# Six blocks of P and four units in flight, results by ScalarE and GpSimd, and the looks at w1 and w2 last

## The chip, the cores and the metric

The kernel runs on one core of a Trainium2 chip. The metric is the device time of one execution in microseconds. A core has TensorE (PE in the profile, its weight loads PEld), VectorE (DVE), ScalarE (ACT), GpSimd (POOL) and SyncE (SP), each working through its own instructions in order, and 16 DMA engines that serve the transfers issued by the queues of SyncE, ScalarE and GpSimd.

## The reference

The input x has 2 batches of 2048 rows of 256. The output is x plus causal attention with one head plus a gated feed-forward network whose weights are ternary (-1, 0 or 1, with one scale for each output):

```python
xn = layernorm(x)
s = where(causal, (xn @ Wq) @ (xn @ Wk).T, -max) * 256 ** -0.5
a = softmax(s) @ (xn @ Wv) @ Wo
h = silu(tlin(xn, w1)) * tlin(xn, w2)       # tlin(x, w) = x @ w.T * s ; 256 -> 1024
h = gelu(tlin(h, h1)); h = gelu(tlin(h, h2))  # 1024 -> 1024
out = x + a + tlin(h, w3)                   # 1024 -> 256
```

## The kernel before

**Two parts.** The kernel computes the attention for all rows first, and the feed-forward network (`ffn_ternary`) after it. In between stands one branch: beside the attention the kernel looks at the weights and counts what would make them not ternary; the sum is `flag`, and a general `ffn` runs where it isn't zero. Numbers are carried as a high and a low half, so that a product takes several matmuls.

**The attention's order.** The rows are cut into 8 blocks n of 512 rows (four for each batch, `NB = 4`), and each block into 4 tiles t of 128 queries. A tile (n, t) meets the key blocks m of its batch up to n. The batch of n = 0..3 is done from the last tile down to the first, that of n = 4..7 upwards, so there are 32 tiles. Python loops write out the order by hand: a list of scoring steps of tile j and a list of weighing steps of tiles some way behind are merged by their TensorE cost (`merged`).

**Scoring.** `score` makes six matmuls for each 512 keys (L401); VectorE moves the scores to SBUF and takes the maximum (L410); when the tile's keys are complete ScalarE takes the exponentials (L422).

**Turning.** P must lie with the keys on the partitions. For most blocks VectorE transposes 32x32 blocks of up to 8 x 128 keys, a *unit* of two key blocks (`turn_blocks`, L292), SyncE stores them to DRAM (d), and four transfers fetch them back in the turned order (`fetch_blocks`, L304) into a tile e; there are 2 such tiles. `turn` then casts the high half of one block (ScalarE, L460) and subtracts for the low half (L462, on VectorE for even m, on GpSimd for odd m) into a tile pT of the pool `ptp`, which holds `LEAD + 2` = 4 of them. Short units go through TensorE transposes instead (L466). `weigh_steps` turns blocks up to `LEAD` = 2 ahead of the one being weighed; `fetch_units` fetches a unit when its first block is turned.

**Weighing.** `weigh` accumulates P times V over a tile's blocks in one PSUM tile po of two halves: one matmul of 512 columns for each 128 keys with the high half of P (L480) and one of 256 with the low half (L485). There are two po. After the last block VectorE sums up and inverts the denominators, ScalarE scales the second half (y, L495), VectorE scales the first and adds y (r, L499), and SyncE stores r of a whole block n (L504).

**Keys and norms.** For the second batch `start_keys` has GpSimd apply the norm (L320), 16 instructions of 128x256 between about 75 and 101 us; `keys` then casts on ScalarE (L338) and subtracts on GpSimd (L339).

**The looks.** `beside(cost)` lets one step of a second list, `looks`, go each time TensorE has been given some cost of work. The list holds, in this order before the change: w1 and w2 (`low`: rounding into w1_sb and w2_sb by GpSimd, L134, then VectorE L558 and ScalarE L560), for each of four pairs of chunks of h1 the sums of factors (VectorE L153) and two `odd` (ScalarE's Abs L565 and VectorE's L567, 128x1024 each), then h2 and parts of w3. When the list is empty, the flag is made by one matmul and copied (L742 to L745). At the end `values_load` (L1173) and the branch (L1174) stand on all engines.

**The feed-forward network.** Each product of 1024 x 1024 factors is done with seven products of half the size instead of eight (`STEPS`). TensorE has eight PSUM banks in two sets of four (`ps_tiles` and `own`); `banks(k)` hands out a set as a whole (k = 4) or as a pair. L172 is the gated product of w1 and w2, L181 and L186 its evictions into f and its halves, L848 the products of h1 and h2.

Of the kernel before, what the change touches and what calls it, by code (L numbers as in the profile page):

```python
# [20 lines left out]
P = 128  # L21
TB = 512
# [10 lines left out]
LOOKS_FROM = 3  # L33
LEAD = 2
WARM = 14

# [28 lines left out]
def attn_ffn_kernel(  # L65
# [123 lines left out]
    with ExitStack() as actx:  # L189
# [6 lines left out]
        sp = actx.enter_context(tc.tile_pool(name="sp", bufs=3))  # L196
        bp = actx.enter_context(tc.tile_pool(name="bp", bufs=2))
        ptp = actx.enter_context(tc.tile_pool(name="ptp", bufs=LEAD + 2))
        small = actx.enter_context(tc.tile_pool(name="small", bufs=4))
# [3 lines left out]
        xs, rstds, ks, qs, vs = {}, {}, {}, {}, {}  # L203
        turns = {"ps": 0, "b": 0, "q": 0}

# [4 lines left out]
        def bank():  # L210
            return in_turn("ps", ps_tiles)

        def load_x(n):
# [40 lines left out]
        def weights_product(name, aT, b, factor):  # L254

            r = cp.tile([P, DC, 2, D], F32R, name=name)
            for c in range(DC):
                ps = bank()
                for d in range(DC):
                    nc.tensor.matmul(  # L260
                        out=ps[:, :D], lhsT=aT[:, d, ts(c, P)], rhs=b[:, d, :],
                        start=(d == 0), stop=(d == DC - 1),
                    )
                f = rp.tile([P, D], F32, tag="y", name=f"wf_{name}_{c}")
# [47 lines left out]
        def start_keys(n):  # L312
            xt = xs.pop(n)
            if n not in rstds:
                mv = cp.tile([P, NT, 2], F32, name=f"mv_{n}")
                stats(xt, mv, n)
                rstds[n] = root(mv, NT, str(n))
            rstd, off = rstds[n]
            for t in range(NT):
                nc.gpsimd.tensor_scalar(  # L320
                    xt[:, t, :], xt[:, t, :], rstd[:, t : t + 1], off[:, t : t + 1],
                    ALU.mult, ALU.add,
                )
            return xt
# [113 lines left out]

        def fetch_units(until, more):
            while units and (more or until not in fetched):  # L440
                more = more and until not in fetched
                n, t, u, k, d = units.pop(0)
                e = bp.tile([P, UK * P], F32, tag="e", name=f"e_{n}_{t}_{u}")[:, : k * P]
                fetched[n, t, u] = fetch_blocks(d, k, e)

        def turn(n, t, m):
# [3 lines left out]
            w = tiles * P  # L450
            pT = ptp.tile([P, 2, TB], F32R, tag="pT", name=f"pT_{n}_{t}_{m}")
            state[n, t][m] = pT
            if by_blocks(n, t, m):
                u, at = divmod((m - first) * NT, UK)
                fetch_units((n, t, u * UK), at == 0)
                src = fetched[n, t, u * UK][:, ds(at, tiles)]
                hi, lo = (
                    pT[:, a, :w].rearrange("p (k i q) -> p k i q", k=tiles, q=Q) for a in range(2)
                )
                nc.scalar.copy(hi, src)  # L460
                engine = nc.gpsimd if m % 2 else nc.vector
                engine.tensor_tensor(lo, src, hi.bitcast(F32), ALU.subtract)  # L462
                return
# [5 lines left out]
            hi_lo(pT[:, 0, :w], pT[:, 1, :w], pt[:, :w])  # L469

        def weigh(n, t, m):
            first = n - n % NB
            st = state[n, t]
# [15 lines left out]
            if m == n:  # L489
# [3 lines left out]
                nc.vector.reciprocal(inv, total)  # L493
                y = rp.tile([P, D], F32, tag="y", name=f"y_{n}_{t}")
                nc.scalar.activation(y, st["po"][:, 1, :], AF.Copy, scale=inv)  # L495
                if n not in attn:
                    attn[n] = rp.tile([P, NT, D], F32, tag="r", name=f"r_{n}"), []
                r, made = attn[n]
                nc.vector.scalar_tensor_tensor(  # L499
                    r[:, t, :], st["po"][:, 0, :], inv, y, ALU.mult, ALU.add  # L500
                )
                made.append(t)
                if len(made) == NT:
                    nc.sync.dma_start(out=r_d[n], in_=r.rearrange("p t d -> p (t d)"))  # L504
                del state[n, t]
# [8 lines left out]
        def weigh_steps(g, until):  # L514

            steps = []
            while g < len(blocks) and blocks[g][0] <= until:
                while turned[0] <= min(g + LEAD, len(blocks) - 1) and (
                    turned[0] <= g or blocks[turned[0]][0] <= until + 1
                ):  # L520
                    b = blocks[turned[0]]
                    steps.append((0 if by_blocks(*b[1:]) else 2 * TB, lambda b=b: turn(*b[1:])))
                    turned[0] += 1
                _, n, t, m = blocks[g]
                steps.append((6 * TB if m < n else 6 * P * (t + 1), lambda b=blocks[g]: weigh(*b[1:])))
                g += 1
# [67 lines left out]
        def item_factors(src, f, c):  # L594
# [3 lines left out]
                (1500, lambda t: store_sums(f, c)),  # L598
                (1500, lambda t: odd(t[0])),
                (3000, lambda t: odd(t[1])),  # L600
# [118 lines left out]
        j = -1  # L719
        checked = False  # L720
        while until < len(tiles) - 1:
# [16 lines left out]
            merged(a, b, beside)  # L738
            if not looks and not checked:
                checked = True  # L740
                most = small.tile([P, 1], F32, tag="most", name="most")
                nc.vector.reduce_max(most, low_bits[:, : looked[0]], axis=AX.X)  # L742
                pf = bank()
                nc.tensor.matmul(out=pf[:1, :1], lhsT=most, rhs=ones, start=True, stop=True)
                nc.vector.tensor_copy(flag, pf[:1, :1])  # L745

        assert checked
        last_quarter = [bank(), bank()]
# [3 lines left out]
    def ffn_ternary(actx):  # L752
# [467 lines left out]
```

## Time and profile before

| what | value |
|---|---|
| median of 3 runs | 872.24 us (872.12 to 873.47) |
| the profiled execution | 871.0 us, of which the span is 869.1 us |
| mean granted TensorE clock | 0.993 |
| TensorE busy | 851.9 us, 98% of the span |
| VectorE, ScalarE, GpSimd busy | 645.9, 498.6 and 236.1 us |
| attention until the first gated product of the last step | to 280.74 us |

Times in the profile are microseconds from the start of the span. A group is named by its line, engine, operation and tiles, as in `L499 DVE ... r<-po,inv,y`. "Releaser" (<-) is what ended the idle time before an instruction. Successive matmuls overlap, so the mean duration of one in the profile is longer than its share of TensorE: the starts of the 512-column matmuls lie 0.227 us apart.

### The profile page before, as it was taken

To read this page: it belongs to the slowest core of one execution; us is meant where nothing else is said; L and a number is where in the kernel's file an instruction comes from. 1 tells how busy PE (TensorE), PEld (TensorE's weight loads), DVE (VectorE), ACT (ScalarE), POOL (GpSimd) and SP (SyncE) were. 2 spreads that over 40 slices of the span, in tenths; PEclk is the share of its full clock that TensorE was granted. 3 is DMA by queue.
4 is the path that set the end of the run, shared out by engine and by line. 5 is a ranking of instruction groups with operands and counts; after the bars stand their busy time and mean duration, and the time that the engine had idled before them with its cause. 6 is when DMAs were issued, how large, how long until landed. Compare 5 with 4: busy or idle time off the path is not lost.

```text
span 869.1 us, 12231 instructions
## 1 busy us (share of the span) xinstructions
PE 851.9 (98%) x4280; PEld 720.8 (83%) x4280; DVE 645.9 (74%) x1127; ACT 498.6 (57%) x881; POOL 236.1 (27%) x180
## 2 busy tenths in 40 slices
PE   8999989999999999999999999999999999999997
PEld 5988778887888878888988888988888898888887
DVE  6698686895875797996596596579468648848764
ACT  2546555754556375676257586536657635557671
POOL 4012634101211666550142050025024003502300
PEclk8999999999999999999999999999999999999999
DMA  8876799775792997854234444432444431144411
GB/s 294 342 243 192 224 328 288 275 230 186 235 321 72 388 395 271 325 193 146 98 123 144 144 144 146 146 121 99 146 145 146 146 135 60 49 145 146 146 49 53
DMA packets 62678, 162.52 MB, mean 187 GB/s; under 512 B 6544, under 2 KB 36368, under 8 KB 53264
## 3 DMA queue, kind: packets, MB, share of 16 engines
q1 hardware_dynamic: 56048, 141.73, 46.9%
q10 hardware_dynamic: 5472, 15.73, 5.6%
q0 software_dynamic: 1088, 4.19, 1.2%
q8 instruction: 36, 0.59, 0.3%
q14 instruction: 34, 0.28, 0.1%
HBM read 120.21 MB, written 47.71 MB: 193 GB/s over the span
## 4 chain that ended last, share of the span: by engine, by line
PE 83%; DVE 7%; DMA 5%; issue 2%; ACT 2%; SPq 1%; POOL 0%; ACTq 0%; DVEq 0%; POOLq 0%
PE ps_own L848 23%; PE ps L848 22%; PE ps L401 8%; PE po L480 5%; PE ps L172 5%; PE ps_own L172 4%; PE ps_own L1009 4%; PE ps L1009 4%; PE po L485 3%; PE ps L357 2%; DMA e<-d 2%; PE ps L373 2%; DVE f_w_B L181 1%; DMA stg<-in_ffn_w_w 1%; DVE h_T L186 1%
## 5 line engine op out<-in xcount | busy, mean ns | idle before, releaser
L401 PE MATMUL ps<-k,q 128*128 128x512 f32 (+3 forms) x480 | 109.1, 367 | 1.7 <-DVE s L410 1.1
L401 PEld LDWEIGHTS ps<-k,q 128*128 128x128 f32 x480 | 81.6, 189 | 14.2 <-DVE s L410 1.5
L480 PE MATMUL po<-v,pT 128*128 128x512 f32 x272 | 80.1, 405 | 4.1 <-DVE r L499 2.5
L462 POOL TENSOR_TENSOR pT<-e,pT 128x512 fp32r<-128x512 f32 (+3 forms) x30 | 35.9, 1197 | 154.1 <-ACT pT L460 103.2
L869 ACT ACTIVATE k_h_u<-k_h_u,h_s_sb 128x512 f32<-128x512 f32 x64 | 45.9, 723 | 37.3 <-DVE k_h_u L868 36.7
L980 POOL TENSOR_TENSOR rt<-rt,xt 128x1024 f32<-128x1024 f32 x8 | 21.5, 2698 | 165.1 <-issue 114.6
L480 PEld LDWEIGHTS po<-v,pT 128*128 128x128 f32 x272 | 48.4, 192 | 12.1 <-issue 2.7
L828 POOL TENSOR_TENSOR k_h_u<-k_h_p,k_h_u 128x512 f32<-128x512 f32 x16 | 23.2, 1453 | 125.5 <-ACT q L185 108.8
L422 ACT ACTIVATE s<-s,low 128x1024 f32<-128x1024 f32 (+7 forms) x48 | 42.9, 896 | 23.7 <-DVE low L416 23.6
L460 ACT CAST pT<-e 128x512 fp32r<-128x512 f32 (+3 forms) x60 | 32.6, 573 | 39.3 <-DMA e<-d 24.5
L410 DVE TENSOR_SCALAR_CACHE_REDUCE s<-ps 128x512 f32<-128x512 f32 (+3 forms) x80 | 46.9, 597 | 5.2 <-PE ps L401 4.6
L485 PEld LDWEIGHTS po<-v,pT 128*128 128x128 f32 x272 | 43.0, 191 | 5.9
L485 PE MATMUL po<-v,pT 128*128 128x256 f32 x272 | 46.4, 284 | 0.0
L186 DVE TENSOR_TENSOR q<-k_h_u,q 128x512 fp32r<-128x512 f32 x32 | 45.9, 1462 | 0.0
L887 POOL TENSOR_TENSOR k_h_p<-f_h_B,k_h_p 128x512 f32<-128x512 f32 x16 | 34.4, 2181 | 21.2 <-DVE h_h_T L186 21.2
L292 DVE STREAM_TRANSPOSE b<-s 128x1024 f32<-128x1024 f32 (+3 forms) x30 | 33.5, 1126 | 8.4 <-ACT s L422 7.6
L462 DVE TENSOR_TENSOR pT<-e,pT 128x512 fp32r<-128x512 f32 x30 | 24.8, 827 | 18.2 <-ACT pT L460 14.3
L172 PE MATMUL ps<-xh,w_sb 128*128 128x512 f32 x144 | 35.9, 391 | 0.0
L828 POOL TENSOR_TENSOR f_w_B<-f_w_B,f_w_B 128x512 f32<-128x512 f32 x16 | 27.0, 1705 | 32.4 <-DVE f_w_B L181 32.4
L868 DVE TENSOR_TENSOR k_h_u<-ps_own,k_h_u 128x512 f32<-128x512 f32 x32 | 21.7, 686 | 18.5 <-PE ps_own L848 18.5
L869 ACT ACTIVATE k_h_p<-k_h_p,h_s_sb 128x512 f32<-128x512 f32 x32 | 23.1, 723 | 20.9 <-DVE k_h_p L868 20.8
L848 PE MATMUL ps<-q,w_h_A 128*128 128x512 f32 x128 | 31.7, 395 | 1.9 <-DVE f_w_B L181 1.7
(177 smaller groups left out, 2202.4 us busy)
## 6 DMA issues: line engine op xcount, KB each, us to landing
w_h_S<-factors_h SPq DMA_DIRECT2D x32, 1024.0 KB, 4.7
w_h_A<-factors_h SPq DMA_DIRECT2D x24, 1024.0 KB, 4.7
d<-b SPq DMA_DIRECT2D x18, 512.0 KB, 3.8
e<-d SPq DMA_DIRECT2D x72, 128.0 KB, 4.0
xT_d<-k SPq DMA_DIRECT2D x8, 1024.0 KB, 8.3
stg<-in_ffn_h_w ACTq DMA_DIRECT2D x16, 512.0 KB, 6.3
x<-in_attn_x SPq DMA_DIRECT2D x16, 256.0 KB, 6.4
factors_h<-xh SPq DMA_DIRECT2D x4, 1024.0 KB, 5.4
```

What stands on the lines that cost most here:

```text
L172: nc.tensor.matmul(out=p, lhsT=w[:, c, ts(o, P)], rhs=xh[:, c, a, :], start=(c == 0 and a == 0), stop=(c == DC - 1 and a == 1),)
L186: nc.vector.tensor_tensor(r[:, 1, :], f, r[:, 0, :].bitcast(F32), ALU.subtract)
L401: nc.tensor.matmul(out=ps[:, :w], lhsT=qs[n][:, c, a, ts(t, P)], rhs=ks[m][:, c, b, :w], start=(k == 0), stop=(m < n and k == 3 * DC - 1),)
L410: marks["DVE"] = nc.vector.tensor_scalar(st["s"][:, ds(at, w)], ps[:, :w], 1.0, None, ALU.mult, ALU.max, accum_out=st["tops"][:, m - first ...
L422: marks["ACT"] = nc.scalar.activation(st["s"][:, at], st["s"][:, at], AF.Exp, bias=low, accum_out=st["sums"][:, u // UK : u // UK + 1],).ins
L462: engine.tensor_tensor(lo, src, hi.bitcast(F32), ALU.subtract)
L480: nc.tensor.matmul(out=st["po"], lhsT=pT[:, 0, ts(j, P)], rhs=vs[m][:, j, :, :], start=(m == first and j == 0), stop=False,)
L485: marks["PE"] = nc.tensor.matmul(out=st["po"][:, 0, :], lhsT=pT[:, 1, ts(j, P)], rhs=vs[m][:, j, 0, :], start=False, stop=(m == n and j == ...
L828: nc.gpsimd.tensor_tensor(B["B12"][i], B["B22"][i], B["B12"][i], ALU.subtract)
L848: nc.tensor.matmul(out=out[o], lhsT=w[:, c, ts(o, P)], rhs=sets[right][c][:, a, :], start=(start and c == 0 and a == 0), stop=(c == HK - 1 ...
L869: nc.scalar.activation(C[k][o], r[o] if r else banks[o], AF.Gelu, scale=s[:, at : at + 1])
L1009: nc.tensor.matmul(out=ys[t][:, :D], lhsT=h[c][:, a, ts(t, P)], rhs=w3_sb[:, c, :], start=(c == 0 and a == 0), stop=(c == HC - 1 and a == 1),)
```

## The change

- `LEAD_BLOCKS = 4`: blocks that are turned through DRAM may be turned four ahead of the weighing; the others keep `LEAD` = 2.
- pT rotates over six tiles: four of the pool, and two pieces of w2_sb's memory. e rotates over four: two of its own, and two pieces of w1_sb's memory. From tile (6, 0) on w1_sb and w2_sb are left alone: the two e tiles serve as pT, and the memory of x as e.
- `fetch_units` keeps up to four units fetched or on their way, instead of fetching on need.
- Results: ScalarE scales both halves of po with one instruction of 128x512 into two neighbouring slots of r (five slots), and GpSimd adds the halves. VectorE's instruction L499 is gone.
- `start_keys` for the second batch has ScalarE apply the norm instead of GpSimd.
- The looks at w1 and w2, with their loads and roundings, come after the sums of the last pair of chunks of h1; the pacing ahead of the first `odd` of a pair is 6000 instead of 1500.
- The flag is made by `judge`, ahead of the very last `weigh`, instead of when the list of looks is empty.
- In the feed-forward network a set of banks that is handed out as a whole begins with the pair that was not handed out last.

```diff
+LEAD_BLOCKS = 4
...
-        bp = actx.enter_context(tc.tile_pool(name="bp", bufs=2))
-        ptp = actx.enter_context(tc.tile_pool(name="ptp", bufs=LEAD + 2))
+        ptp = actx.enter_context(tc.tile_pool(name="ptp", bufs=1))
...
+        pT_tiles = [ptp.tile([P, 2, TB], F32R, name=f"pT_{i}") for i in range(4)]
+        e_tiles = [ptp.tile([P, UK * P], F32R, name=f"e_{i}") for i in range(2)]
+        w_memory = [
+            [w.rearrange("p c h -> p (c h)")[:, ts(i, UK * P)] for i in range(2)] for w in (w1_sb, w2_sb)
+        ]
+        WIDE = (N - 2, 0)
+
+        def pT_tile(n, t):
+            more = e_tiles if (n, t) >= WIDE else w_memory[1]
+            tile = in_turn("pT", pT_tiles + more)
+            return tile if len(tile.shape) == 3 else tile.rearrange("p (a t) -> p a t", a=2)
+
+        def e_tile(n, t):
+            if (n, t) >= WIDE:
+                return xp.tile([P, NT, D], F32, tag="x", name=f"e_{n}_{t}").rearrange("p t d -> p (t d)")
+            return in_turn("e", e_tiles + w_memory[0]).bitcast(F32)
...
             for t in range(NT):
+                if n >= NB:
+                    with tc.issue_after(marks["ACT"]):
+                        nc.scalar.activation(
+                            xt[:, t, :], xt[:, t, :], AF.Identity,
+                            scale=rstd[:, t : t + 1], bias=off[:, t : t + 1],
+                        )
+                    continue
                 nc.gpsimd.tensor_scalar(
...
-        def fetch_units(until, more):
-            while units and (more or until not in fetched):
-                more = more and until not in fetched
+        def fetch_units():
+            while units and len(fetched) < 4:
                 n, t, u, k, d = units.pop(0)
-                e = bp.tile([P, UK * P], F32, tag="e", name=f"e_{n}_{t}_{u}")[:, : k * P]
-                fetched[n, t, u] = fetch_blocks(d, k, e)
+                fetched[n, t, u] = fetch_blocks(d, k, e_tile(n, t)[:, : k * P])
...
+                if at + tiles == fetched[n, t, u * UK].shape[1]:
+                    del fetched[n, t, u * UK]
...
+        def judge():
+            most = small.tile([P, 1], F32, tag="most", name="most")
+            nc.vector.reduce_max(most, low_bits[:, : looked[0]], axis=AX.X)
+            with tc.issue_after(marks["PE"]):
+                pf = bank()
+                nc.tensor.matmul(out=pf[:1, :1], lhsT=most, rhs=ones, start=True, stop=True)
+            nc.vector.tensor_copy(flag, pf[:1, :1])
+
         def weigh(n, t, m):
+            if (n, t, m) == (N - 1, NT - 1, N - 1):
+                judge()
...
-                y = rp.tile([P, D], F32, tag="y", name=f"y_{n}_{t}")
-                nc.scalar.activation(y, st["po"][:, 1, :], AF.Copy, scale=inv)
...
-                nc.vector.scalar_tensor_tensor(
-                    r[:, t, :], st["po"][:, 0, :], inv, y, ALU.mult, ALU.add
-                )
+                up = n < NB
+                two = r[:, ds(t, 2), :]
+                nc.scalar.activation(two, st["po"], AF.Copy, scale=inv)
+                nc.gpsimd.tensor_tensor(two[:, int(up), :], two[:, 0, :], two[:, 1, :], ALU.add)
...
-                while turned[0] <= min(g + LEAD, len(blocks) - 1) and (
-                    turned[0] <= g or blocks[turned[0]][0] <= until + 1
-                ):
+                while turned[0] < len(blocks):
                     b = blocks[turned[0]]
+                    lead = LEAD_BLOCKS if by_blocks(*b[1:]) else LEAD
+                    if turned[0] > g and (turned[0] > g + lead or b[0] > until + 1):
+                        break
...
-                (1500, lambda t: odd(t[0])),
+                (6000, lambda t: odd(t[0])),
...
-        for src, dst in ((w1, w1_sb), (w2, w2_sb)):
-            for c in range(src.shape[1]):
-                item_low(src[:, c, :], dst[:, c, :])
...
             item_factors(h1, factors["h1"], c)
+            if c == HK - 1:
+                for src, dst in ((w1, w1_sb), (w2, w2_sb)):
+                    for i in range(DC):
+                        item_low(src[:, i, :], dst[:, i, :])
...
-            if not looks and not checked:
-                checked = True
...
-        half, pair = [1], [1, 0]
+        half, pair = [1], [0, 1]
...
+            two = [four[:2], four[2:]]
             if k == 4:
-                return four
+                return two[1 - pair[half[0]] % 2] + two[pair[half[0]] % 2]
             pair[half[0]] += 1
-            return four[2:] if pair[half[0]] % 2 == 0 else four[:2]
+            return two[pair[half[0]] % 2]
```

More of the change, by code (lines that the diff above doesn't have):

```diff
@@ L203, in attn_ffn_kernel @@
         xs, rstds, ks, qs, vs = {}, {}, {}, {}, {}
-        turns = {"ps": 0, "b": 0, "q": 0}
+        turns = {"ps": 0, "b": 0, "q": 0, "pT": 0, "e": 0}
         def in_turn(key, tiles):
@@ L211, in bank @@
             return in_turn("ps", ps_tiles)
+        pT_tiles = [ptp.tile([P, 2, TB], F32R, name=f"pT_{i}") for i in range(4)]
[3 more added lines that the diff above has]
+        ]
+        assert DC * H == 2 * UK * P and UK * P == 2 * TB == NT * D
+        WIDE = (N - 2, 0)
[7 more added lines that the diff above has]
+            return in_turn("e", e_tiles + w_memory[0]).bitcast(F32)
         def load_x(n):
@@ L263, in weights_product @@
                     )
-                f = rp.tile([P, D], F32, tag="y", name=f"wf_{name}_{c}")
+                f = rp.tile([P, NT + 1, D], F32, tag="r", name=f"wf_{name}_{c}")[:, 0, :]
                 nc.scalar.mul(f, ps[:, :D], factor)
@@ L450, in turn @@
             w = tiles * P
-            pT = ptp.tile([P, 2, TB], F32R, tag="pT", name=f"pT_{n}_{t}_{m}")
+            pT = pT_tile(n, t)
             state[n, t][m] = pT
@@ L454, in turn @@
                 u, at = divmod((m - first) * NT, UK)
-                fetch_units((n, t, u * UK), at == 0)
+                fetch_units()
                 src = fetched[n, t, u * UK][:, ds(at, tiles)]
+                if at + tiles == fetched[n, t, u * UK].shape[1]:
+                    del fetched[n, t, u * UK]
                 hi, lo = (
@@ L469, in turn @@
             hi_lo(pT[:, 0, :w], pT[:, 1, :w], pt[:, :w])
+        def judge():
+            assert not looks
+            most = small.tile([P, 1], F32, tag="most", name="most")
[4 more added lines that the diff above has]
+            nc.vector.tensor_copy(flag, pf[:1, :1])
         def weigh(n, t, m):
+            if (n, t, m) == (N - 1, NT - 1, N - 1):
+                judge()
             first = n - n % NB
@@ L493, in weigh @@
                 nc.vector.reciprocal(inv, total)
-                y = rp.tile([P, D], F32, tag="y", name=f"y_{n}_{t}")
-                nc.scalar.activation(y, st["po"][:, 1, :], AF.Copy, scale=inv)
                 if n not in attn:
-                    attn[n] = rp.tile([P, NT, D], F32, tag="r", name=f"r_{n}"), []
+                    attn[n] = rp.tile([P, NT + 1, D], F32, tag="r", name=f"r_{n}"), []
                 r, made = attn[n]
-                nc.vector.scalar_tensor_tensor(
-                    r[:, t, :], st["po"][:, 0, :], inv, y, ALU.mult, ALU.add
-                )
+                up = n < NB
+                two = r[:, ds(t, 2), :]
+                nc.scalar.activation(two, st["po"], AF.Copy, scale=inv)
+                nc.gpsimd.tensor_tensor(two[:, int(up), :], two[:, 0, :], two[:, 1, :], ALU.add)
                 made.append(t)
                 if len(made) == NT:
-                    nc.sync.dma_start(out=r_d[n], in_=r.rearrange("p t d -> p (t d)"))
+                    assert made == sorted(made, reverse=up)
+                    nc.sync.dma_start(out=r_d[n], in_=r[:, ds(int(up), NT), :].rearrange("p t d -> p (t d)"))
                 del state[n, t]
@@ L719, in attn_ffn_kernel @@
         j = -1
-        checked = False
         while until < len(tiles) - 1:
@@ L738, in attn_ffn_kernel @@
             merged(a, b, beside)
-            if not looks and not checked:
-                checked = True
[L741 to L747, printed above, removed]
         last_quarter = [bank(), bank()]
```

## The prediction

> **What bounds the kernel now.** I read the page first: its busy shares, the 40 slices and the chain that ended last. Then the waits of TensorE alone in the attention stage, the timeline of VectorE at the longest of them, a table by stage, and last the groups by line with their shapes kept apart, for the durations.
>
> ```profile
> PE 851.9 (98%) x4280; PEld 720.8 (83%) x4280; DVE 645.9 (74%) x1127; ACT 498.6 (57%) x881; POOL 236.1 (27%) x180
> ...
> PE   8999989999999999999999999999999999999997
> ...
> PE 83%; DVE 7%; DMA 5%; issue 2%; ACT 2%; SPq 1%; POOL 0%; ACTq 0%; DVEq 0%; POOLq 0%
> ```
>
> TensorE is busy for 98% of the span. The change leaves its matmuls as they are and only reorders them, so what can be gained is TensorE's idle time and its slow clock, and nothing else. The waits of TensorE from 60 to 285 us (total, times, longest):
>
> ```profile
> PE po L480 <- DVE r L499: 2.5, 1, 2.5
> PE po L480 <- ACT pT L460: 1.5, 2, 0.9
> PE ps L401 <- DVE s L410: 1.1, 2, 0.6
> PE ps L401 <- DVE v L252: 0.6, 1, 0.6
> ```
>
> That is 5.7 us in six waits. The largest is one event at 110.5 us. VectorE's timeline there (start, duration):
>
> ```profile
> 107.29 1.46 DVE L567 SCALAR_TENSOR_TENSOR stg<-stg 128x1024 f32<-128x1024 f32 x1 [0.79 <-ACT stg L565]
> ...
> 109.28 1.23 DVE L292 STREAM_TRANSPOSE b<-s 128x1024 f32<-128x1024 f32 x1
> 110.44 2.05 DVE L567 SCALAR_TENSOR_TENSOR stg<-stg 128x1024 f32<-128x1024 f32 x1
> ...
> 112.43 0.47 DVE L499 SCALAR_TENSOR_TENSOR r<-po,inv,y 128x256 f32<-128x256 f32 x1
> 112.83 1.35 DVE L462 TENSOR_TENSOR pT<-e,pT 128x512 fp32r<-128x512 f32 x1
> ```
>
> The result instruction L499, which frees po, stands behind a transpose and a look at the weights (L567). Its end at 112.90 lets TensorE go on at 113.05. The table by stage (length, then busy us of PE, PEld, DVE, ACT, POOL, then PEclk, DMA share, GB/s):
>
> ```profile
> 100.00:110.00 10.00, 9.06 (x54) 7.91 (x53) 6.79 (x11) 6.76 (x15) 2.72 (x4) 1.00 1.08 314
> 110.00:120.00 10.00, 7.47 (x32) 6.10 (x31) 10.00 (x22) 5.74 (x12) 6.69 (x4) 0.83 1.05 351
> 120.00:140.00 20.00, 20.00 (x119) 17.69 (x118) 15.95 (x43) 12.02 (x26) 6.21 (x5) 1.00 0.95 288
> 300.00:320.00 20.00, 18.86 (x82) 14.96 (x82) 19.87 (x21) 9.86 (x19) 15.09 (x11) 1.00 1.03 386
> ```
>
> The granted clock falls to 0.83 for the 10 us that hold the wait: 10 x 0.17 = 1.7 us more. From 300 to 320 us VectorE itself is full (19.87 of 20).
>
> **The change part by part.** The forecast is worked out against the profiled execution: 871.0 us, span 869.1, 1.9 us around it. It lies 1.24 us below the median of 872.24; I assume the median moves by as much as the span.
>
> *Results by ScalarE.* VectorE loses 32 instructions of 0.474 us (L499): 15.2 us. ScalarE's 32 of 128x256 (L495, 0.471) become 32 of 128x512 from PSUM; the nearest row, L180, takes 0.688: 32 x 0.22 = +7.0 us. po is then free after ScalarE alone. The wait at 110.5 us goes, 2.53 us, and the slow clock behind it, 1.7 us: **-4.2**. It goes whole only if nothing else is late there: in the old order the low half of pT (L462, 112.83, 1.35 us) is, and without the longer lead below only about 1 us would be won. The Trainium skill's page "TensorE: Matmul & The Clock Gate", Part 1, has the clock halve only after an idle window of about 3.4 us. Since 2.53 us of idling sufficed here, I go by the row. By the rule alone the slow clock is not this wait's doing, and the sum would be 1.7 us poorer.
>
> *Lead of four blocks, four e units, six pT.* Casts wait less for their transfer, and the two waits on pT L460 at 89.3 and 104.7 us (0.57 and 0.94) fall inside the lead: four blocks of 1.40 us each (the starts of L480's groups at 277.94 and 279.34), 5.6 us of TensorE's work: **-1.5**. Bounds: 0, if the DMA engines (share 1.08 and 1.05 between 100 and 120 us) deliver no sooner however early SyncE asks; -1.5, all of it. An e transfer took up to 7.8 us there, more than one block and less than a unit of two blocks plus the lead (8.4), so I take the whole.
>
> *The other VectorE waits* (1.1 + 0.6 us) stand behind the same looks. VectorE is 15.2 us lighter, but the two L567 of a pair (now a 6000-cycle pacing before the first) still lie next to each other in places in the new order: half, **-0.85**. Bounds 0 and -1.7.
>
> *Bank order in the FFN.* The first product of an input takes the pair that was released first, one matmul (0.227 us) earlier. It can help at the waits on f_w_B L181 at 458.5, 605.1 and 751.5 us (0.17, 0.38, 0.17 of idling): 0.17 + 0.23 + 0.17 = **-0.6**. At 306 to 323 us VectorE's chain sets the pace (row 300:320), so nothing there.
>
> *ScalarE's new load.* Besides the 7.0 us, 16 normalisations (128x256) come from GpSimd (L320, 0.660 each). ScalarE's nearest rows are 0.399 (cast, L460) and 0.471 (L495): 16 x 0.44 = 7 us, nearly all between 75 and 150 us. Between 100 and 150 us ScalarE was busy 29.0 of 50 us; about 12 us are added there. Counted in the new program order by these durations, tiles 8 to 15 hold 34.4 us of ScalarE against 33.5 us of TensorE: 0.9 us too much, and a clump (four normalisations, 1.9 us, or two Abs of 1.05) ahead of a cast. Bounds 0 (the lead covers it) and 4 us (both clumps twice uncovered); I take 0.9 plus half a clump, **+1.9**.
>
> *GpSimd's new load.* It loses 16 x 0.660 = 10.4 us and gets 32 two-input adds of 128x256; the L462 rows give 0.585 (128x128) to 0.958 (128x256), so 19 to 31 us. It was busy for 57 of the 225 us from 60 to 285, so it isn't a bound; its odd splits queued behind an add are covered by the lead. But it slows VectorE: L462 takes 0.799 on VectorE beside GpSimd where L252, the same shape from PSUM, takes 0.684; and the L567 that met GpSimd's L339 took 2.05 instead of 1.22. For 32 adds that is between 32 x 0.115 = 3.7 and 32 x 0.83 = 27 us of VectorE, against the 15.2 removed. I go by the L462 row, as near in size, and put one collision on the path: **+0.9**, bounds 0 and 3. The page "SBUF — State Buffer", section "SBUF: two separate sides", speaks against the change: a VectorE instruction with two SBUF inputs and a GpSimd one share an exclusive port pair, and the loser is blocked for the whole instruction. The 0.115 us of the L462 row says that most don't meet; by the rule at its worst 31 us of blocking would eat the 15.2 us freed and the forecast would be no gain.
>
> *Late flag.* The flag's matmul stands ahead of the last weigh. Behind it TensorE has that block (1.40) and eight gated matmuls of 0.227 (1.81): 3.2 us. Beside it run the copy (0.14), the register load (0.49) and a branch (0.09), about 0.9 with the hops: hidden. ScalarE's last result is 0.2 us longer, and SyncE's last store of r waits for GpSimd's add before the branch, 0.7 us later; the xh1t load behind it is late by the same for the VectorE chain from 290 us on: **+0.4**, bounds 0 and 1.4.
>
> *Looks at w1 and w2 last* move 2 MB to about 215 to 245 us, where the DMA share was 0.64, and GpSimd's four roundings (1.05 each) to before the first gated product: nothing, as long as the last P is out of that memory in time; 2 us (two roundings) if not.
>
> Sum: -4.2 - 1.5 - 0.85 - 0.6 + 1.9 + 0.9 + 0.4 = -3.95, so **-4.0**: span 865.1, this execution 867.0, median 868.2.
>
> *Waits that are new.* ScalarE's result also waits for GpSimd's add of the tile before (it writes the neighbouring slot); queued behind it are the casts of pT. That add is a whole tile old (5 us and more), so 0; without this cover, an add's 0.96. GpSimd's add waits for ScalarE, with odd splits behind it, and SyncE's store of r for the add, half a us later than for L499, with e fetches and d stores behind it: both lie inside the lead and the four units, 0; uncovered, half a us at each of eight stores.
>
> **The rivals.**
>
> *A: the gain is eaten, no change.* With L499 gone, the low half of pT on VectorE, or the transfer of e at a DMA share of 1.0, is late at the same place. For it: L462 stands directly behind L499 at 112.83, and ScalarE waited 24.5 us for e in this stage. Against it: five of six waits are under 1 us, less than the lead. Of 4.2 + 1.5 only 1 + 0.75 are won: -1.75 - 0.85 - 0.6 + 1.9 + 0.9 + 0.4 = 0.0, 872.2.
>
> *B: ScalarE becomes the bound, slower.* Place: tiles 8 to 15, 110 to 150 us. ScalarE works in order, and from 85 to 165 us it idled 14.5 us for e and 3.0 us for VectorE's maxima. If the 33.5 us of these tiles keep their share of that, 17.5 x 33.5 / 80 = 7.3, it needs 34.4 + 7.3 = 41.7 us, 8.2 more than TensorE. If the lead of 5.6 us stands in full, 2.6 us show and 1.7 of slow clock; if ScalarE never gets ahead, 8.2 and 3.4. The mean is 8.0 in place of the 1.9: -3.95 + 6.1 = +2.1, 874.3. It decides from 5.9 us of waits and slow clock on. Against it: the longer lead is what should shrink ScalarE's waits for e.
>
> *C: the changed hand-over costs.* The flag's cover fails or w1's memory is released late: +1 to +2 on the forecast, 869.7.
>
> **How the numbers follow.** Forecast 0.52, A 0.18, B 0.24, C 0.06. The low end is every gain in full (4.2 + 1.5 + 1.7 + 0.6 = 8.0) without a charge, 864.2, and half a us for a wait that I overlooked: 863.7. The high end is B with half a us more, 874.8. The forecast's own range is 864.2 to 870.4. About 0.2%, 1.7 us, is what a measurement of this kernel can tell from no change. Faster: the forecast, a sixth of A and most of C, 0.60. Same: two thirds of A and a little of B, 0.15. Slower: the rest, 0.25.
>
> **What would show it.** Right: no wait of TensorE on results of about 2.5 us near 110 us, PEclk 1.00 in 110:120, no wait on the casts of pT over 0.3 us, the first gated matmuls about 3 us earlier than at 280.74 us. B shows as waits of TensorE on pT casts between 105 and 150 us, with ScalarE over 90% busy. A shows as a wait on the low halves (L462's successor) or on ScalarE waiting for e near 110 us. C shows as idling of TensorE around the branch. An FFN shorter or longer by over 1 us from its first matmul to the end would make my terms for it wrong.

## The result and the profile after

The changed kernel takes 874.06 us (median of 20 runs, 871.46 to 878.03), the kernel before 871.14 in its 20 runs (869.59 to 875.17): ratio 1.0036, 95% interval 1.0025 to 1.0047, so about 3 us slower where 4 us faster was forecast, and the interval excludes no change. The profiled execution is 873.67 us with a span of 871.9, against 871.0 and 869.1.

The page of the changed kernel, the rows that answer to those of before:

```profile
PE 852.1 (98%) x4280; PEld 721.7 (83%) x4280; DVE 638.7 (73%) x1095; ACT 511.5 (59%) x897; POOL 257.0 (29%) x196
...
PE   8999989999898999999999999999999999999997
...
PE 73%; DMA 14%; DVE 5%; ACT 2%; issue 2%; SPq 2%; ACTq 0%; POOL 0%; DVEq 0%; POOLq 0%
```

TensorE's work is the same. In the chain that ended last, 14% of the span now goes through transfers (5% before). The waits of TensorE in the attention stage (60 to 290 us), whole answer:

```profile
PE po L520 <- ACT pT L271: 4.1, 1, 4.1
PE ps L173 <- ACT b L181: 2.8, 1, 2.8
PE po L520 <- ACT pT L488: 2.3, 1, 2.3
```

All six waits of before are gone, as forecast; three others have come, all of them on ScalarE, and all longer than any old one but that of 110 us (2.53). They stand at 123.8, 222.7 and 268.0 us. The table by stage (columns as before):

```profile
100.00:110.00 10.00, 10.00 (x55) 8.66 (x54) 8.75 (x19) 7.05 (x14) 2.99 (x3) 1.00 0.59 210
110.00:120.00 10.00, 10.00 (x57) 8.48 (x57) 9.02 (x21) 4.76 (x7) 3.36 (x2) 1.00 0.98 292
120.00:140.00 20.00, 15.93 (x79) 13.61 (x78) 12.83 (x33) 13.77 (x28) 5.97 (x7) 0.83 0.85 298
300.00:320.00 20.00, 18.65 (x83) 15.08 (x82) 19.84 (x19) 9.20 (x16) 16.81 (x12) 1.00 1.02 390
```

The slow clock has moved from 110:120 to 120:140, and it lasts twice as long (0.83 over 20 us instead of 10); a second spell follows the wait at 222.7 us (0.83 in 220:230). What is in front of the first wait is seen on ScalarE:

```profile
116.47 0.68 ACT L540 ACTIVATE r<-po,inv 128x512 f32<-128x512 f32 x1
...
121.58 1.14 ACT L365 CAST k<-x 128x512 fp32r<-128x512 f32 x2 [4.43 <-DMA x<-d_x]
122.63 1.04 ACT L449 ACTIVATE s<-s,low 128x896 f32<-128x896 f32 x1
...
123.67 1.08 ACT L342 ACTIVATE x<-x,off,rstd 128x256 f32<-128x256 f32 x2
...
127.60 0.25 ACT L271 CAST pT<-pt 128x128 fp32r<-128x128 f32 x1
```

ScalarE stands still for 4.43 us, because the cast of the second batch's keys (L365) waits for their transfer. The cast that TensorE needs (L271) takes 0.25 us and comes six microseconds after that wait. The two others have the same form:

```profile
224.30 1.14 ACT L488 CAST pT<-e 128x512 fp32r<-128x512 f32 x2 [6.24 <-DMA e<-d]
...
264.68 0.62 ACT L488 CAST pT<-e 128x512 fp32r<-128x512 f32 x1 [6.19 <-DMA e<-d]
```

At 222 us TensorE needs that very cast. At 268 us it needs a gate (L181), which comes at 269.99, behind this cast, a result, two exponentials and a table load.

Where the time went can be added up from the starts of the matmuls: what lies between two starts beyond 0.227 us (512 columns), 0.172, 0.118 or 0.111 (384, 256, 128). From 60 to 287 us TensorE loses 11.7 us before and 16.2 after; from 287 us to the end 4.6 and 2.9. That is +4.5 - 1.7 = +2.8, the difference of the two spans. So the feed-forward part won more than forecast, and the attention stage lost. The first gated matmuls of the last step come at 285.36 us instead of 280.74, where 3 us earlier was to be a sign of a right forecast.

Cut by place, with the changed kernel's two other profiled executions (two of the runs below) beside it:

| TensorE loses, us | before | changed kernel |
|---|---|---|
| 85 to 165 us | 7.9 | 7.4, 9.5 and 7.4 |
| 165 to 205 us | 1.1 | 0.3, 0.3 and 0.3 |
| 205 to 287 us | 2.5 | 8.2, 10.2 and 11.8 |

From 85 to 165 us the new wait eats what the old ones give back. The loss itself stands at 205 to 287 us, the stage to which the looks at w1 and w2 moved. Single executions of one order of instructions differ by up to 4 us here, so only large differences count.

### The profile page after: what moved, and what is told of

It is laid out like the page before. It is cut to its first block, busy times and chain, and to the rows that moved or that the text cites. A ratio compares the mean times of both kernels' runs of the same rounds, so it can differ in the third digit from the quotient of the medians.

```text
span 871.9 us, 12243 instructions
## 1 busy us (share of the span) xinstructions
PE 852.1 (98%) x4280; PEld 721.7 (83%) x4280; DVE 638.7 (73%) x1095; ACT 511.5 (59%) x897; POOL 257.0 (29%) x196
## 4 chain that ended last, share of the span: by engine, by line
PE 73%; DMA 14%; DVE 5%; ACT 2%; issue 2%; SPq 2%; ACTq 0%; POOL 0%; DVEq 0%; POOLq 0%
PE ps_own L884 23%; PE ps L884 22%; PE ps L173 6%; DMA d<-b 6%; PE ps_own L173 5%; PE ps_own L1045 4%; PE ps L1045 4%; DMA e<-d 3%; PE ps L428 3%; PE po L520 2%; SPq L324 2%; PE ps L400 2%; DMA stg<-in_ffn_h_w 2%; PE po L525 1%; DVE b L312 1%
## 5 line engine op out<-in xcount | busy, mean ns | idle before, releaser
L520 PE MATMUL po<-v,pT 128*128 128x512 f32 x182 | 55.5, 409 | 6.3 <-ACT pT L271 4.1
L541 POOL TENSOR_TENSOR r<-r 128x256 f32<-128x256 f32 x32 | 30.6, 959 | 56.1 <-ACT r L540 56.1
L520 PEld LDWEIGHTS po<-v,pT 128*128 128x128 f32 x182 | 32.8, 194 | 11.6 <-ACT pT L271 4.3
L173 PEld LDWEIGHTS ps<-xh,w_sb 128*128 128x128 f32 x144 | 26.5, 188 | 8.4 <-ACT b L181 3.1
L490 POOL TENSOR_TENSOR pT<-e,pT 128x512 fp32r<-128x512 f32 (+2 forms) x12 | 15.0, 1248 | 61.8 <-ACT pT L488 59.5
L525 PEld LDWEIGHTS po<-v,pT 128*128 128x128 f32 x182 | 29.0, 191 | 4.2 <-DVE pT L490 0.2
L187 DVE TENSOR_TENSOR h_h_B<-f_h_B,h_h_B 128x512 fp32r<-128x512 f32 x32 | 21.4, 717 | 14.8 <-ACT h_h_B L186 14.8
```

The lines of the kernel that those rows point to most:

```text
L173: nc.tensor.matmul(out=p, lhsT=w[:, c, ts(o, P)], rhs=xh[:, c, a, :], start=(c == 0 and a == 0), stop=(c == DC - 1 and a == 1),)
L187: nc.vector.tensor_tensor(r[:, 1, :], f, r[:, 0, :].bitcast(F32), ALU.subtract)
L520: nc.tensor.matmul(out=st["po"], lhsT=pT[:, 0, ts(j, P)], rhs=vs[m][:, j, :, :], start=(m == first and j == 0), stop=False,)
L525: marks["PE"] = nc.tensor.matmul(out=st["po"][:, 0, :], lhsT=pT[:, 1, ts(j, P)], rhs=vs[m][:, j, 0, :], start=False, stop=(m == n and j == ...
```

## The experiments

The rivals, once the traces had been compared, were: the norm on ScalarE is late (N), the longer lead clogs ScalarE's queue (L), the reload of xh0 holds SyncE up (S), and the moved looks cost (M). Each experiment ran on one chip together with the kernel before, and its ratio is against that. The changed kernel itself was run three times in this way (1.0036; 1.0063, interval 1.0046 to 1.0079; 1.0038), so a difference of up to 0.3% between experiments on different chips says nothing.

**One part of the change undone, or one size changed**

*The norm back on GpSimd.*

```diff
-                if n >= NB:
-                    with tc.issue_after(marks["ACT"]): nc.scalar.activation(...)
-                    continue
```

> The changed kernel with the norm of the second batch back on GpSimd. In the changed kernel's trace the norms ran on ScalarE from 105.3 us (before: on GpSimd from 89.4), the transposed x was stored at 109.5 us (before 94.7), and ScalarE waited 4.4 us for it ahead of the wait of 4.1 us at 123.6 us. Theory N (the norm behind ScalarE's queue is late, and its four instructions stand ahead of a cast that TensorE needs): the wait near 124 us goes with its spell of slow clock, 4.1 + 2.8 = about 6 to 7 us, so about -5 to -7 us against the changed kernel, about 868, faster than before; the waits near 222 and 268 us stay. Theory F (the store of factors of 1 MB issued at 112.2 us, half a us ahead of the fetch of x, is what delays x): the wait near 124 us stays, over 2 us, and the time within 1.5 us of 874.

Measured: 888.72 us, ratio 1.0192 (1.0176 to 1.0208). N fell in this form. TensorE's waits, the first three:

```profile
PE ps L173 <- ACT b L181: 5.1, 1, 5.1
PE po L513 <- ACT pT L481: 4.0, 2, 2.6
PE ps L173 <- DVE s L430: 2.2, 1, 2.2
```

Beside GpSimd's adds the norm is worse placed than on ScalarE, by about 1.3% (the changed kernel on the same chip was 1.0063). In the kernel before, the trace has these norms on GpSimd from 89.4 to 101.1 us.

*A lead of two.* `LEAD_BLOCKS = 2`.

> The changed kernel with a lead of two blocks instead of four; the rotation over six pT and four e stays. Theory L (the longer lead puts casts that still wait for their transfer earlier into ScalarE's queue, and the exponentials and gates behind them come late): ScalarE's waits for e of over 6 us near 218 and 258 us shrink, the wait of TensorE on the gate near 268 us (2.8 us) goes, and perhaps the one near 222; 3 to 6 us below 874. Rival (the transfers are late in themselves, the lead covers what it can): the same waits or more, some of the small waits on casts of before (0.6 to 0.9 us) back, 874 to 878.

Measured: 877.06, 1.0062 (1.0046 to 1.0078), with the same three waits (4.8, 2.6 and 2.6 us). The changed kernel on the same chip was 1.0063 (next run). L fell, and with four units in flight the longer lead is worth nothing that can be measured.

*The reload of xh0 later in the list.*

```diff
-            if c == HK - 1:
-                steps.append((0, lambda t: load_xh0()))
...
+                        # as a second step of the last look at w2
+                        item_low(src[:, i, :], dst[:, i, :], [(0, lambda t: load_xh0())] if last else ())
```

> The changed kernel with the reload of xh0 put behind the last look at w2 instead of directly behind the last store of factors of h1. Theory S (at 205 us SyncE waits 5.0 us for that store to land before it may reload xh0, and the stores and fetches of P queued behind it, and 1 MB in front of them, come late): the wait near 222 us (2.3 us and 1.6 us of slow clock) goes, -3 to -4 us, about 870.5; the waits near 124 and 268 stay. Rival (2 MB of w1 and w2 loaded in this stage fill the DMA engines): the wait near 222 us stays over 1.5 us.

The scheduler of the build, which fixes the order of each engine's instructions, put the reload back where it was, and the order of instructions on every engine is that of the changed kernel. So this says nothing on S; it is a second sample of the changed kernel, 877.29 us, 1.0063.

*The reload of xh0 held back on SyncE's queue:* the same edit, and `with tc.issue_after(marks["SP"])`, the mark being the latest store of d.

> The changed kernel with the reload of xh0 held back behind the stores of d that are emitted before the last look at w2 is done, some 35 us later on SyncE's queue. Theory S (the reload stands 5 us before the two stores of d at 210 us and moves 1 MB in front of them): the wait near 222 us (2.3 us and 1.6 of slow clock) goes, about 4 us below the changed kernel. Rival (w1 and w2 on their way fill the DMA engines): the wait stays over 1.5 us.

Measured: 878.51, 1.0081 (1.0056 to 1.0107). The stores of d went out at 209.7 us without the reload and landed 2.6 and 3.0 us later. In the changed kernel the reload of xh0 (1 MB) goes out at 210.1 us just ahead of them, and they take 7.3 and 8.7 us. The wait near 222 us shrank to 1.1 us by the starts of the matmuls. But the waits near 124 (3.5 us) and 268 (3.5 us) stayed, and VectorE's maxima gave two new ones (2.6 us). S was right on the main cause of this one wait and wrong on the price: other waits took over, and from 205 to 287 us TensorE lost 13.3 us in this execution.

*Results back on VectorE.*

```diff
-                nc.scalar.activation(two, st["po"], AF.Copy, scale=inv)
-                nc.gpsimd.tensor_tensor(two[:, int(up), :], two[:, 0, :], two[:, 1, :], ALU.add)
...
+                nc.scalar.activation(y, st["po"][:, 1, :], AF.Copy, scale=inv)
+                nc.vector.scalar_tensor_tensor(r[:, t, :], st["po"][:, 0, :], inv, y, ALU.mult, ALU.add)
```

> The changed kernel with the results as before: ScalarE scales one half (128x256), VectorE scales and adds the other; nothing on GpSimd. Theory of the prediction (the new results free po early and win about 4 us): the wait of po on VectorE comes back somewhere, 876 to 878. Rival (ScalarE is the engine that is late now, and GpSimd's adds slow VectorE): ScalarE is 7 us lighter, the waits near 124 and 268 us shrink, 870 to 873.

Measured: 879.73, 1.0097 (1.0081 to 1.0112), against 1.0063 for the changed kernel on the same chip. Inside the changed kernel the new results win about 0.3%, 3 us: VectorE is late instead, twice for the low half of a P turned on TensorE.

```profile
PE po L525 <- DVE pT L272: 5.0, 2, 2.5
```

*Keys turned one tile earlier.* `TURN_KEYS = [7, 9, 11, 13]`.

> The changed kernel with the keys of the second batch turned one tile earlier (TURN_KEYS 7, 9, 11, 13 instead of 8, 10, 12, 14). Theory N (the norm on ScalarE is late, x lands late, and ScalarE stands before TensorE's cast): the wait near 124 us (4.1 us and 2.8 of slow clock in the changed kernel) goes or falls under 1.5 us, 4 to 7 us below the changed kernel (ratio to before 0.996 to 1.001). Rival (the store of factors ahead of the fetch of x, or ScalarE's sum of work): the wait stays over 3 us, ratio 1.003 to 1.007.

Measured: 890.11, 1.0205 (1.0174 to 1.0235). The wait near 124 us went, and one of 3.7 us came at 108, for the same reason: the scheduler moved the cast of the keys ahead too.

```profile
107.39 1.14 ACT L365 CAST k<-x 128x512 fp32r<-128x512 f32 x2 [6.48 <-DMA x<-d_x]
```

The four fetches of x were issued from 99.0 us on, and x was usable at 107.4. So turning the keys earlier doesn't help: the order is fixed ahead, ScalarE works it off in sequence, and a cast that is put where its transfer hasn't landed stops everything behind it. In the changed kernel the fetches of x go out at 112.7 to 115.5 us, directly behind a store of factors (1 MB, 112.2 us), and take 5.6 to 7.0 us; in the kernel before the first three left at 97.3 to 98.2 us, ahead of that store, and took 2.7 to 4.6. That the store is what delays them was not isolated.

*Two units fetched ahead:* `len(fetched) < 2`.

> The changed kernel with at most two units fetched ahead instead of four. Theory M: no difference to the changed kernel beyond 0.2%. Rival (SyncE's early fetches go in front of x and of the stores of d and make them late): 3 to 5 us below the changed kernel, the wait near 124 us under 2 us.

Measured: 876.32, 1.0055 (1.0036 to 1.0073); the changed kernel on the same chip (an empty line added) 875.09, 1.0038 (1.0022 to 1.0054). No difference that these intervals allow to tell. What was expected of this second build of the changed kernel, and its three longest waits:

> The changed kernel itself (an empty line is added), so that the other runs of this call are held against it on the same chip: ratio to before 1.003 to 1.007, waits of TensorE near 124, 222 and 268 us.

```profile
PE po L521 <- ACT pT L272: 3.7, 1, 3.7
PE ps L174 <- ACT b L182: 3.7, 1, 3.7
PE po L521 <- ACT pT L489: 2.6, 1, 2.6
```

The three waits are there again in this execution.

*The pacing back at 1500.*

> The changed kernel with the pacing ahead of the first odd of a pair at 1500 again instead of 6000; the late looks at w1 and w2 stay. If the pacing is what costs in the moved looks: 3 to 6 us below the changed kernel, ratio 0.997 to 1.000. If it is their order (sums of h1 in the stage of 85 to 165 us, w1 and w2 beside the last tiles): ratio 1.003 or more, waits near 222 and 268 us stay.

Measured: 878.98, 1.0088 (1.0070 to 1.0107). The pacing isn't what costs in the looks: the time is not below the changed kernel's. Whether 6000 is the better value is not shown, as the changed kernel did not run on this chip (1.0036 to 1.0063 elsewhere). The waits near 222 and 268 us, which were expected to stay, moved: one of 4.4 us stands at 246, one of 1.0 at 273.

*The old order of banks.*

> The changed kernel with the order of banks as before. If the bank order wins 3 us here as it did in the kernel before: ratio 1.007, by the starts of its matmuls 2 to 3 us more lost from 290 us on. If it wins only the 0.6 us of the prediction: ratio 1.004 to 1.005.

Measured: 878.77, 1.0093 (1.0068 to 1.0118). From 290 us on TensorE loses 6.7 us instead of 2.9 to 3.0 in the three executions of the changed kernel; one of the waits is 2.4 us long, and a spell of half clock follows it. So the bank order wins some 3 us or more here too, as far as experiments on different chips can be compared.

**One part alone, on the kernel before**

*The bank order* (the edit of `banks` in the change).

> The kernel before with the new order of banks in the feed-forward network alone. The sum put -0.6 us on it. The changed kernel's trace has 1.4 us of waits of TensorE from 300 us to the end, the kernel before 2.3, and by the starts of the matmuls 2.9 against 4.6 us of lost time. Theory (the bank order alone does that): -0.6 to -1.7 us, ratio 0.998 to 0.9993, the waits on f_w_B near 458, 605 and 751 us gone and those at 306 to 322 us fewer. Rival (the shift of the stage's start did it): no difference, the waits stay.

Measured: 867.89, 0.9966 (0.9946 to 0.9985): faster than both kernels. Of the waits on f_w_B and h_T after 300 us (2.3 us in five) one is left:

```profile
PE ps L849 <- DVE f_w_B L181: 0.4, 1, 0.4
```

By the starts of the matmuls 1.9 us are lost there instead of 4.6. The win of 3.0 us is that of the medians; the profiled execution, 871.28, is one of the slower ones and loses 2.6 us more in the attention stage.

*The results*, *the norm*, *the looks* (order and pacing), each alone:

> The kernel before with the results by ScalarE and GpSimd alone; the norms stay on GpSimd. The prediction: the wait of 2.5 us on L499 goes, about 1 us is won because the low half of pT is next, 871.2. Theory Q (GpSimd's adds wait for TensorE's end of a tile, and what is queued behind them on GpSimd, norms and odd halves, comes late, as in the run with the norm back on GpSimd): +2 to +10 us, waits of TensorE on casts and on low halves.

> The kernel before with the norm of the second batch on ScalarE alone. Theory N (on ScalarE the norm comes late, behind exponentials, and x with it): a wait of TensorE of 2 to 5 us between 105 and 130 us, +3 to +7 us. Rival (the norm's engine makes no difference of its own): within 1.5 us of 872.

> The kernel before with the looks at w1 and w2 after the sums of h1 and the pacing of 6000 alone. Theory M (the moved transfers, sums earlier, 2 MB later beside the last tiles, make e late near 222 us and the gate late near 268): +2 to +5 us with waits at these places. Rival (order of looks alone is harmless; what is late is ScalarE's and SyncE's own new work): within 1.5 us of 872, the wait near 110 us still there or moved.

Measured: results 874.84, 1.0032 (1.0012 to 1.0052); norm 872.80, 1.0026 (1.0006 to 1.0047); looks 874.43, 1.0048 (1.0026 to 1.0070). Each costs by itself. With the results alone TensorE no longer waits for VectorE to free po, but for a low half of pT (1.1 us), q (2.6) and scores (1.6), and for 2.4 us at its first wait after the branch; by the starts of the matmuls 14.0 and 6.8 us are lost in the two parts instead of 11.7 and 4.6. With the looks alone the sums of h1 come 26 to 44 us earlier (the stores of factors at 74.0, 109.2, 161.6 and 205.2 us instead of 104.9, 153.6, 187.5 and 240.5), into the stage where P is moved. The profiled execution, 872.04, is the fastest of the twelve and shows only half of the cost: 13.8 us lost from 60 to 287 us instead of 11.7.

**Halves of the change**

*The engines' half:* the kernel before with results, norm and bank order. *The transfers' half:* the changed kernel with results and norm as before.

> The half of the change that concerns engines: the kernel before with results by ScalarE and GpSimd, norms by ScalarE and the new bank order; two e, four pT, lead of two, looks and flag as before. If the costs add (results +2.8, norms +2.3, banks -3.0): +2 us, 873. If results and norms belong together (the norm no longer stands behind GpSimd's adds): 867 to 869, below the bank order alone or equal to it. If ScalarE is overloaded by the two together: 875 or more, waits on casts between 105 and 150 us.

> The half of the change that concerns transfers: the changed kernel with results on ScalarE and VectorE and norms on GpSimd as before; lead of four, borrowed memory, four units, late looks at w1 and w2, late flag and bank order stay. Theory of two halves that need each other (the norm had to leave GpSimd only because of the adds, and the longer lead pays when po comes free early): 872 to 876 with waits on L499's successor. Theory M (the moved looks cost by themselves, about 4 us, the bank order wins 3): 871 to 873, waits near 124 us gone. Rival (the transfers' half is the good one): 866 to 869.

Measured: engines' half 871.57, 0.9985 (0.9967 to 1.0003); transfers' half 881.21, 1.0113 (1.0082 to 1.0144). Without the bank order's 0.34% results and norm cost about 0.2% together (some 0.3% either way) instead of the 0.6% of the two runs alone; that they belong together is likely by this, not shown. The loss is in the other half, although its bank order is the new one too.

*The engines' half with the looks of the change.*

> The kernel before with results by ScalarE and GpSimd, norms by ScalarE, the new bank order, and the looks at w1 and w2 late with the pacing of 6000; no borrowed memory, no longer lead, flag as before. Without the looks this was 0.9985 of before. Theory M (the moved looks are what costs): 1.003 to 1.008, the level of the changed kernel, so that four units and six blocks are worth nothing. Rival (the units, the borrowed memory and the lead are what costs): 0.997 to 1.001.

Measured: 883.75, 1.0127 (1.0100 to 1.0154). Against the engines' half (0.9985) the moved looks alone cost 1.4%, 12 us. VectorE and, behind it, ScalarE and TensorE in this run:

```profile
105.11 1.40 DVE L153 TENSOR_TENSOR xh<-stg,stg 128x512 fp32r<-128x512 f32 x1 [4.54 <-DMA stg<-in_ffn_h_w]
106.43 1.23 DVE L292 STREAM_TRANSPOSE b<-s 128x1024 f32<-128x1024 f32 x1
...
110.66 0.11 DVE L423 TENSOR_REDUCE low<-tops 128x1 f32<-128x2 f32 x1
110.69 0.54 DVE L252 TENSOR_TENSOR pT<-pt,pT 128x384 fp32r<-128x384 f32 x1
```

```profile
110.80 1.15 ACT L429 ACTIVATE s<-s,low 128x1024 f32<-128x1024 f32 x1 [4.74 <-DVE low L423]
```

```profile
111.28 1.01 PE L492 MATMUL po<-v,pT 128*128 128x256 f32 x3 [3.12 <-DVE pT L252]
```

It is the same form on another engine: a sum of factors stands on VectorE before its weights have landed, 4.54 us, and a transpose of P, a maximum and the low half that TensorE needs stand behind it. But this place isn't where the 12 us are. From 85 to 165 us TensorE loses 10.5 us here and 10.2 in the engines' half without the looks; from 165 to 205 it is 8.3 against 0.3, and from 205 to 287 it is 7.3 against 3.1. There it is again ScalarE that stands for a fetch of P:

```profile
189.07 0.82 ACT L467 CAST pT<-e 128x512 fp32r<-128x512 f32 x2 [8.25 <-DMA e<-d]
...
189.74 1.61 PE L487 MATMUL po<-v,pT 128*128 128x512 f32 x3 [1.87 <-ACT pT L467]
```

Borrowed memory, lead, four units and the late flag, which the looks make room for, then win 1.0127 - 1.0038 = 0.9% back, 8 us: less than the looks cost.

*The bank order and the norm.*

> The kernel before with the new bank order and the norms by ScalarE, results as before. Norms alone were 1.0026 of before, banks alone 0.9966. If they add: 0.999. If what the norm cost alone (waits on f_w_B of 2.7 us after the branch against 1.7) is mended by the bank order: 0.995 to 0.997, as good as the bank order alone or better.

Measured: 870.10, 0.9997 (0.9982 to 1.0013). By the medians they add (0.9966 and 1.0026 give 0.9992); the bank order doesn't mend what the norm costs. The best kernel found is the one before with the new bank order alone.

## Why the prediction was wrong

The time lies in the range, on the other side of no change than the forecast, within a third of a microsecond of rival B (874.3). B had the right engine, the right place (waits on casts of pT between 105 and 150 us) and the slow clock after a gap; its cause was not quite right. ScalarE wasn't full: in 120:140 it was busy for 13.8 of 20 us, and it stood still for a transfer ahead of the cast. Two of the three waits (222.7 and 268.0 us) stand outside B's place. That the times agree so closely is in part luck: the kernel before ran at 871.14 instead of 872.24, so B's +2.1 stands against +2.9 measured, and terms that are off by 2 to 7 us each way cancel. The sum, term by term:

| term | forecast | shown |
|---|---|---|
| results by ScalarE and GpSimd | -4.2 | alone +2.8 (1.0032); inside the changed kernel about -3 |
| lead, four units, memory (waits on casts) | -1.5 | the old waits are gone; lead of two or two units: no difference that can be told; together with the late flag -8 against the looks that make room for them |
| VectorE's other waits | -0.85 | gone in the changed kernel; three on scores (1.7 us) are back where the results are undone |
| bank order | -0.6 | -3.0 alone (0.9966) |
| ScalarE's new load | +1.9 | norm alone +2.3 (1.0026) |
| GpSimd's new load | +0.9 | not isolated; no wait of TensorE in the changed kernel is put down to GpSimd |
| late flag | +0.4 | no wait of TensorE at the branch; not isolated |
| looks at w1 and w2 last | 0 | +4.2 alone (1.0048), +12 on the engines' half |

**The step that failed is the last: "looks at w1 and w2 last ... nothing".** The prediction priced the moved looks by the bytes they move and by the DMA share of the stage that receives w1 and w2, and named only a late release of memory as what they could cost. The share was misread: 0.64 is that of 200 to 285 us in the kernel before, and from 215 to 245 us, where the 2 MB were to go, it was 0.81 already (columns as before):

```profile
215.00:245.00 30.00, 29.99 (x166) 25.82 (x165) 27.03 (x64) 19.23 (x36) 6.33 (x5) 1.00 0.81 247
200.00:285.00 85.00, 83.93 (x447) 71.59 (x446) 61.40 (x143) 50.63 (x95) 15.69 (x12) 1.00 0.64 201
```

The runs show +4.2 us for the moved looks alone and +12 on the engines' half, and in the changed kernel TensorE loses 8.2 to 11.8 us from 205 to 287 us instead of 2.5. In the six traces without the moved looks this stage loses 1.5 to 5.0 us; with them it is 3.3 (alone), 7.3 (on the engines' half) and 8.2 to 16.8 in the changed kernel and its variants. One piece is shown: the reload of xh0, which follows the sums of h1 and so came 35 us earlier too (210.1 instead of 244.8 us), stood ahead of two stores of d and made most of the wait at 222.7 us (1.1 us of it is left with the reload held back). The sums of h1 with their weights went into 85 to 165 us, where the DMA share had been 0.92; their cost there was put at nothing too. No run moved the sums, the reload and the looks at w1 and w2 one by one, so how the cost divides among them is open. And work of a look that waits for a transfer was not seen as something that blocks its engine's queue.

**The second is what follows a removed wait.** All six old waits went, and 4.5 us more were lost. The prediction asked of each wait what is next in the old order; but the new order is another one, and its waits stand elsewhere. What is next was to be looked for in the new order: each instruction that waits for a transfer (casts of keys, casts of P, sums), how long before it that transfer is issued, and what TensorE needs stands behind it. Trace rows for that were there. The 7.8 us that the prediction took for the longest fetch of e is one at 192 us; in the same trace fetches issued at 115.9 and 247.3 us took 8.8 and 8.9, more than the 8.4 us that the lead was to cover.

**The third is a size.** In the feed-forward part I counted one matmul (0.227 us) for the bank order and nothing before 323 us, as VectorE is full there. But for the first input the last bank was asked for after 19 matmuls of the product in the old order and after 24 in the new: five matmuls, 1.1 us. By the starts of the matmuls the first input loses 2.3 us before, at three places (306.6, 308.9 and 322.0 us), and 0.6 with the new bank order alone: 1.7 us won where nothing was forecast. At the three later inputs it is 1.2 us before and 0.5 after: 0.7 us won, about the 0.6 that were counted. That VectorE was full didn't matter, as TensorE waited for one eviction out of it, not for its sum.

Right were: TensorE's old waits go, with the clock of 110:120 at 1.00; the hand-over is hidden (no wait of TensorE between 270.7 and 314 us in the changed kernel); GpSimd's 32 adds take 959 ns each, 30.6 us in all, and TensorE waits for none of them there. (The first of the two old waits on pT stood at 89.7 us, not 89.3; nothing rests on it.)

On the two pages of the Trainium skill that were weighed: the clock fell behind a wait of 4.1 us and behind one of 2.3 us (0.83 in 120:140 and in 220:230), so the window of about 3.4 us in "TensorE: Matmul & The Clock Gate", Part 1, is not a length that the idling has to reach. But the row that the prediction went by isn't a rule either: the wait of 2.77 us at 268.0 us left the clock at 1.00 in 260:270 and 270:280. Between 2.3 and 2.8 us the length alone doesn't decide. The cost of the shared port pair in "SBUF — State Buffer", section "SBUF: two separate sides", was not isolated: L490, VectorE's low half, ran for 1.62 and 1.78 us beside GpSimd's instructions and for 0.69 elsewhere, but no run took one of the two away alone.

What stays open: which part of the moved looks costs, why they cost three times as much on the engines' half as alone, and how much of the 8 us belongs to the borrowed memory and how much to the late flag; no run separated them.

## What to carry to other kernels

An order that is fixed ahead is only as good as its guess of when transfers land: before moving work earlier, list the instructions that wait for a transfer on an engine that works in sequence, and what the critical engine needs behind each. Room that is won by moving other work has to be paid where that work goes, and that is a term of the sum like any other, to be read from the rows of that very stretch and not from the mean of a longer one. A change of many parts is worth taking apart: here the smallest edit, the order in which two pairs of banks are handed out, was the only one of the four parts run alone that won.

## What was not expected of the hardware

A wait of 2.27 us at 222.7 us was followed by TensorE at half rate for some 3.3 us (starts 0.427 us apart instead of 0.227), as 2.53 us had been before, while a wait of 2.77 us at 268.0 us was not (starts 0.23 us apart). And transfers issued by SyncE took far longer to be usable than they did elsewhere in the same trace when others were on their way: 512 KB of d stored at 210.6 us could be read at 217.9, and with the reload held back the store of 209.7 us landed in 2.6; 512 KB of x asked for from 99.0 us on, with the keys turned earlier, were cast at 107.4.
